# A fused transformer block: masked products moved to GpSimd, a count round split between two engines

## Chip, cores and metric

One core of a Trainium2 chip. The metric is the time of one execution on the device in microseconds (us). PE is TensorE (PEld its weight loads), DVE VectorE, ACT ScalarE, POOL GpSimd, SP SyncE.

## What is computed

The reference is two layers over x of shape 8 x 512 x 256; each adds an attention-like and a feed-forward part to a residual. The change touches only the attention of the first layer:

```
q, k, v = heads(xn @ Wq.T), heads(xn @ Wk.T), heads(xn @ Wv.T)      # 16 heads of 64
k, v    = concat(mem_k, k), concat(mem_v, v)                        # 64 memory keys in front
dots    = mix_heads(q @ k.T / 8, pre_proj)                          # heads blended, 16 x 16
dots    = where(key after query + 64, -max, dots)
kth     = top_k(dots, 64)[..., -1]                                  # the 64th largest of each row
attn    = softmax(where(dots < kth, -max, dots))
out     = mix_heads(attn, post_proj) @ v;  out @ Wout.T + bout
```

The rest is a feed-forward part with blockwise FP4 quantisation, then a second layer with a decaying scan (a convolution in the reference), a gated part and an INT4 dense part with a low-rank addition.

## The kernel before

**Tiling.** For each of 8 batches the 512 queries are cut into 8 groups of 64, taken in the order 7, 0, 5, 2, 6, 1, 4, 3. Group g sees up to `64 + 64 (g + 1)` keys. A group is a tile of 128 partitions (16 heads x 8 queries) by 8 blocks (`b`), and block b of group g has `keys(8 g + b) = 64 + 8 (8 g + b + 1)` columns, 72 to 576. The tile lies in a ring buffer `ring`, which holds six groups; a new group's scores may land only when an older group's last use (`turned`, L1299 and L1319) is over.

**Stages of a group.** `scores`: matmuls (L1004), evictions by ACT (L1019), DMAs that spread heads over partitions (L1028, SP's queue), clears by POOL (L1036), a matmul that blends heads (L1047), and ACT's exponentials into the ring (L1055), masked by POOL (L1068, L1070). So the ring holds positive numbers.

`search`: for each row a threshold `cur` is sought that a few less than 64 entries reach. A round counts, block by block, the entries on either side. On ACT a count is a Sign activation with an accumulator (L1085; ACTIVATE and ACTIVATION_READ_ACCUMULATOR are its two records); on DVE a comparison with an accumulator (L1089). `LONG` lists the rounds as (blocks counted on ACT, whether the step is made on POOL): three rounds with all eight blocks on ACT and the step on POOL, two rounds with all on DVE and the step on DVE. The step `narrow` (L1101 to L1147) turns counts into the next threshold with a chain of tiny instructions. ACT's sums are of signs and DVE's of ones; `base` turns the first into an excess over the aim. In a round that both share (`EDGE`, the first two groups of all), DVE's comparison is multiplied by -2 through a third operand `two` (L1091). `LAST` serves the last four groups. The last round's counts become `off`, the number that is still missing.

`soften`: for each block DVE makes a masked product, entries below the threshold and zeros for the others (L1155), and takes its eight largest (MAX8, L1158). `pick` (L1162 to L1169) selects the 64th largest from threshold, those eight and `off`, with a table `slots`. L1182 then zeroes what lies under it and sums the rest; its reciprocal (L1263) scales the mixing matrices on POOL (L1274).

`attend`: matmuls that mix heads and transpose (L1299, L1319), evictions (L1307, L1325), the product with v (L1343), then the output projection (L1367, L1371). Keys (L942), queries (L970) and values (L911) are made once per batch or pair of groups; in the drain the quantised feed-forward part of one batch is begun early (`early_mlp`, `begin_last`).

**Order of work.** Nothing is ordered by the hardware's timing alone: a planner (`Plan`) gets every operation with an engine, a modelled cost, its dependencies and the buffers that it takes and gives (`room`: so many of each name, taken in program order except for some). It plays the operations through; of those that an engine could start at about the same time it takes the one with the earliest due time. The result is the order of instructions on each engine, which is fixed. Due times are set by stage: `due(n, start, end)` spreads a stage's operations between two offsets, in groups, around group n's place on a clock (`DUE`, `START`, `MLP_DUE`, `BEGIN_DUE`). The second layer is planned separately, by the length of the chain behind each operation (its instructions all have line L276).

Of the kernel before, what the change touches and what calls it, by code (L numbers as in the profile page):

```python
# [8 lines left out]
F32 = mybir.dt.float32  # L9
U32 = mybir.dt.uint32  # L10
AF = mybir.ActivationFunctionType
ALU = mybir.AluOpType
# [3 lines left out]
P = 128  # L16
# [6 lines left out]
TOPK = 64  # L23
RB = 8
HH = H // 2
NB = N // RB
GB = 8
# [3 lines left out]
WD = [MEM + GR * (g + 1) for g in range(NG)]  # L31
# [10 lines left out]
def places(order):  # L42
# [16 lines left out]
AIM = LOW + 4.25  # L59
SPAN = 9  # L60

LONG = ((GB, True), (GB, True), (GB, True), (0, False), (0, False))

EDGE = ((GB // 2, False),) * (len(LONG) - 1) + ((0, False),)
LAST = ((GB, True),) * 3 + ((GB, False), (0, False))
# [7 lines left out]
FCH = ((0, 128), (128, 128), (256, 128), (384, 128), (512, 96), (608, 96))  # L73
FKC = len(FCH)
BLK = 16
MLP_DUE = (-6.89, -6.28)
BEGIN_DUE = (-4.57, -3.22)
START = dict(guess=(-7.0, -6.94), wvs=(-3.0, 6.46), out=(-2.39, -0.44), weights=(-6.86, -1.78), stores=(-3.17, 5.9))
DUE = dict(
    tokens=((-5.67, -1.96),),  # L80
    keys=((-4.8, -3.44),),
    queries=((-4.7, 2.49),),
    scores=((-2.64, -2.01), (-2.54, -2.24),),
    search=((6.0, 8.0), (6.0, 7.56),),
    soften=((-2.19, 5.82), (-6.06, -4.32),),
    values=((0.45, 3.36),),
    attend=((2.8, 3.05), (0.76, 6.89),),
    project=((-4.72, 6.69),),
)
FLT_MAX = 3.4028234663852886e38  # L90
MASKED = -1.0e30
# [555 lines left out]
def block_kernel(ctx: ExitStack, tc: tile.TileContext, a: dict, out: bass.AP):  # L647
    nc = tc.nc
# [51 lines left out]
    with ExitStack() as c0:  # L700
        keep = c0.enter_context(tc.tile_pool(name="keep", bufs=1))
# [9 lines left out]
        guess = keep.tile([P, NB], F32, name="guess")  # L711
# [5 lines left out]
        below = keep.tile([P, RB], F32, name="below")  # L717

        slots = keep.tile([P, SPAN], F32, name="slots")
        base = {}  # L720
        for na in sorted({na for na, _ in LONG + EDGE + LAST} - {0}):
            base[na] = keep.tile([P, NB], F32, name=f"base{na}")
        minus = keep.tile([P, GB], F32, name="minus")
        good = keep.tile([P, NB], F32, name="good")
        two = keep.tile([P, 1], F32, name="two")

        wvT = keep.tile([P, DC, H * DH], F32, name="wvT")
        woT = keep.tile([P, HC, D], F32, name="woT")
# [3 lines left out]
        scr = c0.enter_context(tc.tile_pool(name="scr", bufs=1))  # L732
# [7 lines left out]
        rp = c0.enter_context(tc.tile_pool(name="rp", bufs=2))  # L740
        wp = c0.enter_context(tc.tile_pool(name="wp", bufs=2))
# [5 lines left out]
        extra = keep.tile([P, 1840], F32, name="extra")  # L747
        with tc.tile_pool(name="prep", bufs=1) as prep, tc.tile_pool(name="prep_ps", bufs=1, space=PSUM) as pps:
            pl = Plan({})
            r = Straight(nc, pl, True)  # L750
# [81 lines left out]
            r.vector.tensor_scalar(below, cmask, -1.0, 1.0, ALU.mult, ALU.add)  # L832
            r.vector.tensor_scalar(cmask, cmask, MASKED, None, ALU.mult)
            for q in range(SPAN):
                r.gpsimd.memset(slots[:, q : q + 1], 2 * (TOPK - AIM - q))
            for na, to in base.items():
                r.gpsimd.memset(to, -2.0 * AIM)
                for ib in range(NB):
# [1 line left out]
                        r.gpsimd.memset(to[:, ib : ib + 1], keys(ib) - 2.0 * AIM)  # L840
            r.gpsimd.memset(good, 0.0)
            r.gpsimd.memset(minus, -1.0)
            r.gpsimd.memset(two, -2.0)
# [230 lines left out]
        def block(s, g, b):  # L1074
            return s[:, b, : keys(g * GB + b)]

        def count(g, s, cur, raw, b, na):


            on_act = b < na  # L1080
            src = block(s, g, b)
            thr = cur[:, 0, b : b + 1]
            junk = wp.tile([P, WD[-1]], I8, name=f"junk{int(on_act)}")[:, : src.shape[-1]]
            if on_act:
                nc.scalar.activation(  # L1085
                    junk, src, AF.Sign, bias=thr, scale=-1.0, accum_out=raw[:, b : b + 1]
                )
            elif na == 0:
                nc.vector.tensor_scalar(junk, src, thr, 0.0, ALU.is_ge, ALU.add, accum_out=raw[:, b : b + 1])  # L1089
            else:  # L1090
                nc.vector.scalar_tensor_tensor(  # L1091
                    junk, src, thr, two.to_broadcast([P, src.shape[-1]]), ALU.is_ge,
                    ALU.mult, accum_out=raw[:, b : b + 1],
                )

        def excess(eng, to, g, raw, na):

            if na == 0:
                eng.tensor_scalar(to, raw, 2.0, -2.0 * AIM, ALU.mult, ALU.add)
            else:  # L1100
                eng.tensor_tensor(to, base[na][:, g * GB : (g + 1) * GB], raw, ALU.subtract)  # L1101

        def narrow(g, w, k, na, on_pool):
# [46 lines left out]
        def under(g, s, cur, top, b):  # L1150
# [6 lines left out]
            )  # L1157
            nc.vector.max(out=top[:, b, 1:], in_=y)  # L1158

        def pick(cur, top, off, kth):  # L1160
# [35 lines left out]
        def search(pl, g, s, w, deps, rounds):  # L1196

            def begin():
                w["cur"] = cur = st.tile([P, 2, GB], F32, name="cur", bufs=14)
                nc.gpsimd.tensor_copy(cur[:, 0], guess[:, g * GB : (g + 1) * GB])  # L1200

            tail = pl.add("POOL", 0.3, begin, deps)
            for k, (na, on_pool) in enumerate(rounds):
                def open_():
                    w["raw"] = st.tile([P, GB], F32, name="raw", bufs=8)

                counts = []
                tail = pl.add("none", 0.0, open_, [tail])
                for b in range(GB):
                    def one_count(b=b, na=na):  # L1210
                        count(g, s, w["cur"], w["raw"], b, na)

                    n = keys(g * GB + b)
                    counts.append(
                        pl.add("ACT", 0.28 + 0.00083 * n, one_count, deps + [tail]) if b < na else
                        pl.add("DVE", 0.13 + 0.00105 * n, one_count, deps + [tail])
                    )

                def step(k=k, na=na, on_pool=on_pool):
                    if k < len(rounds) - 1:  # L1220
                        narrow(g, w, k, na, on_pool)
                    else:
                        w["off"] = st.tile([P, GB], F32, name="foff", bufs=4)
                        excess(nc.vector, w["off"], g, w["raw"], na)

                last = k == len(rounds) - 1
                tail = pl.add(
                    "POOL" if on_pool else "DVE",
                    0.2 if last else (0.9 if k == 0 else 4.6) if on_pool else 1.8 if k < len(rounds) - 2 else 2.1,
                    step, counts,  # L1230
                )
                deps = []
            return tail

        def soften(pl, g, s, w, tail, seen):

            def top0():
                w["top"] = small.tile([P, GB, SPAN], F32, name="top", bufs=2)

            op = tail  # L1240
            for b in range(GB):
                def un(b=b):
                    if b == 0:
                        top0()
                    under(g, s, w["cur"], w["top"], b)

                n = keys(g * GB + b)
                op = pl.add("DVE", 0.42 + 0.00154 * n, un, [op, tail])
            op = picked = pl.add("DVE", 0.9, lambda: pick(w["cur"], w["top"], w["off"], w["kth"]), [op])
            for b in range(GB):  # L1250
# [250 lines left out]
        def begin_last(pl, guard, ready):  # L1501
# [10 lines left out]


        pl = Plan(dict(
            scr=1, xnT=2, ps_m=3, ps_s=2, ps_a=2, ps_y=1, v=1, q=2, k0=1, k1=1, raw=4, rp=2, at=2, y=1,
            xset=1, xqT=2, hset=1, hT=2,
        ), ("scr", "ps_m", "ps_s", "ps_a", "ps_y"))
        groups = [(b, g) for b in range(B) for g in ORDERS[b]]
# [13 lines left out]


        r = Straight(nc, pl)
        hold = ["at", "at", "y", "ps_a", "ps_a", "ps_y", "xnT"]
        held_ = pl.add("none", 0.0, lambda: None, (), hold)
        banks = [ps_a.tile([P, 512], F32, name="ps_at") for _ in range(2)] + [ps_y.tile([P, 512], F32, name="ps_y")]
# [42 lines left out]
        junk = gates[:, 512:768].rearrange("p (j d) -> p j d", d=DH)  # L1580
# [62 lines left out]
        made = section("weights")  # L1643
# [3 lines left out]
        r.sync.dma_start(mk_d.rearrange("p (c m) -> p c m", m=MEM), kt[:, :, :MEM])  # L1647
        section("stores")
        pl.add("none", 0.0, lambda: None, [made, guessed, v_made, o_made], (), hold)

        kd = {}
        yt, ydone, judged, freed = {}, [], [None, None], {-1: made, -2: v_made, -3: o_made}
        for n, (b, g) in enumerate(groups):
# [15 lines left out]
            s = room(found[n][0], g)  # L1669
            last = n % NG == NG - 1  # L1670
# [4 lines left out]
            w = {}  # L1675
# [360 lines left out]
```

## Time and profile before

| | us |
|---|---|
| three runs: median (lowest to highest) | 2375.78 (2371.23 to 2377.31) |
| the profiled execution, its own time | 2370.63 |
| its span, first to last instruction | 2368.9 |
| first and last L1155 (masked product) start | 149.5, 1802.5 |
| busy PE, DVE, ACT, POOL | 2144.4, 2029.9, 1893.1, 1099.1 |

The mean granted TensorE clock was 0.96. The attention of the first layer takes the span from about 100 to 1820 us; the second layer and most of the feed-forward part follow. A row of the costliest groups reads: line, engine, operation, written and read tiles with shapes, count, then busy us and mean ns of one, then the engine's idle time just before them with what ended it.

### The profile page before, as it was taken

Reading aid. Unit: us, or ns where it says so; the run is one execution under the profiler, and the core shown is the slowest. Engines: PE = TensorE matmul, PEld = TensorE weight load, DVE = VectorE, ACT = ScalarE, POOL = GpSimd, SP = SyncE. Lnnn points to the kernel's source line nnn. Section 1 sums busy time; section 2 is a strip of 40 time slices with the busy share of each in tenths; the row PEclk is TensorE's granted clock in tenths of the full one; section 3 lists DMA queues with packets and bytes.
Section 4 is the critical chain, followed back from the end, with each engine's and each line's share of the span. In section 5 each row is a group of like instructions: output and inputs, shape, how many; then the busy total and the mean of one; then the engine's idle time right before and its main releaser. Section 6 shows DMA issues by size and latency. Waiting matters only on the chain. (4 is left out here: it accounts for less than half of the span.)

```text
span 2368.9 us, 57412 instructions
## 1 busy us (share of the span) xinstructions
PE 2144.4 (91%) x19629; PEld 1522.0 (64%) x19629; DVE 2029.9 (86%) x6462; ACT 1893.1 (80%) x5501; POOL 1099.1 (46%) x2678
## 2 busy tenths in 40 slices
PE   8788999989989999998999999999676889999998
PEld 7346675766767676676767667765455456665566
DVE  6998989988998998898899889979897788778764
ACT  4599999989999998998999899999963456444434
POOL 2424554445545554544455455545554544444330
PEclk9899999999999999999999999999888889999999
DMA  6552333253232424323332422444000310000000
GB/s 187 126 115 52 61 54 67 46 85 60 62 61 58 66 52 85 56 56 61 67 65 49 88 50 68 67 66 96 6 16 25 111 36 18 19 12 16 10 10 18
DMA packets 117156, 137.57 MB, mean 58 GB/s; under 512 B 20059, under 2 KB 102774, under 8 KB 116598
## 3 DMA queue, kind: packets, MB, share of 16 engines
q1 hardware_dynamic: 116854, 133.80, 28.0%
q8 instruction: 158, 2.59, 0.5%
q14 instruction: 144, 1.18, 0.2%
HBM read 27.32 MB, written 15.73 MB: 18 GB/s over the span
## 5 line engine op out<-in xcount | busy, mean ns | idle before, releaser
L1085 ACT ACTIVATE junk<-ring,cur 128x480 int8<-128x480 f32 (+33 forms) x1552 | 885.0, 586 | 11.9 <-POOL cur L1147 9.6
L1089 DVE TENSOR_SCALAR_CACHE_REDUCE junk<-ring,cur 128x520 int8<-128x520 f32 (+7 forms) x976 | 510.3, 540 | 78.2 <-POOL cur L1147 75.9
L1047 PE MATMUL ps_sc<-ring,blend 128*128 128x264 f32 (+50 forms) x1152 | 363.7, 436 | 44.6 <-DMA ring<-raw 20.6
L1319 PE MATMUL ps_at<-mixd,ring 128*128 128x128 f32 x2560 | 353.8, 287 | 22.1 <-POOL mixd L1274 12.5
L1319 PEld LDWEIGHTS ps_at<-mixd,ring 128*128 128x128 f32 x2560 | 320.3, 197 | 61.0 <-POOL mixd L1274 20.5
L1085 ACT ACTIVATION_READ_ACCUMULATOR junk<-ring,cur 128x1 f32 x1552 | 337.2, 217 | 0.0
L1155 DVE SCALAR_TENSOR_TENSOR y<-ring,cur 128x520 f32<-128x520 f32 (+56 forms) x512 | 307.3, 600 | 7.3
L1047 PEld LDWEIGHTS ps_sc<-ring,blend 128*128 128x128 f32 x1152 | 193.3, 195 | 163.6 <-ACT ring L1055 56.5
L1182 DVE SCALAR_TENSOR_TENSOR ring<-ring,kth 128x520 f32<-128x520 f32 (+56 forms) x512 | 280.6, 556 | 1.1
L1158 DVE MAX8 top<-y 128x8 f32<-128x520 f32 (+56 forms) x512 | 255.7, 499 | 17.6
L1019 ACT COPY raw<-ps_mi 128x284 f32<-128x284 f32 (+15 forms) x576 | 223.1, 430 | 38.3 <-DMA ring<-raw 28.6
L1004 PE MATMUL ps_mi<-kt,qT 64*32 64x284 f32 (+15 forms) x4608 | 230.3, 442 | 15.4 <-ACT raw L1019 13.9
L1055 ACT ACTIVATE ring<-ps_sc 128x272 f32<-128x272 f32 (+33 forms) x576 | 229.0, 426 | 16.8 <-PE ps_sc L1047 14.7
L1343 PEld LDWEIGHTS ps_y<-at,v 128*64 128x64 f32 (+1 forms) x6144 | 196.1, 138 | 58.3 <-ACT at L1325 19.8
L1343 PE MATMUL ps_y<-at,v 128*64 128x64 f32 (+1 forms) x6144 | 220.4, 225 | 3.9 <-ACT at L1325 2.8
L1137 POOL TENSOR_TENSOR by<-gap,minus 128x8 f32<-128x8 f32 x124 | 212.7, 1715 | 9.7
L1325 ACT COPY at<-ps_at 128x512 f32<-128x512 f32 x320 | 191.2, 600 | 29.5 <-PE ps_at L1319 28.0
L1101 POOL TENSOR_TENSOR cur<-base,raw 128x8 f32<-128x8 f32 x186 | 46.4, 249 | 329.2 <-ACT junk L1085 326.1
L1274 POOL TENSOR_TENSOR mixd<-mix,rden 128x256 f32<-128x256 f32 x256 | 168.8, 684 | 18.7 <-DVE rden L1263 16.4
L276 PE MATMUL ps_gu<-big,ring 128*128 128x352 f32 x448 | 149.2, 478 | 15.4 <-DVE hid L276 8.4
L1036 POOL MEMSET ring<- 128x56 f32 (+6 forms) x448 | 34.7, 124 | 247.1 <-DMA ring<-raw 244.2
L276 PE MATMUL ps_l<-ring,w 128*128 128x512 f32 (+2 forms) x288 | 124.3, 575 | 21.2 <-DVE u L276 15.7
(306 smaller groups left out, 3889.8 us busy)
## 6 DMA issues: line engine op xcount, KB each, us to landing
ring<-raw SPq DMA_DIRECT2D x32, 288.0 KB
ring<-raw SPq DMA_DIRECT2D x32, 284.0 KB
ring<-raw SPq DMA_DIRECT2D x32, 256.0 KB
ring<-raw SPq DMA_DIRECT2D x32, 252.0 KB
ring<-raw SPq DMA_DIRECT2D x32, 224.0 KB
ring<-raw SPq DMA_DIRECT2D x32, 220.0 KB
ring<-raw SPq DMA_DIRECT2D x32, 192.0 KB
ring<-raw SPq DMA_DIRECT2D x32, 188.0 KB
```

The costliest lines, as they stand in the source:

```text
L276: call = lambda: fn(*a, **k)
L1004: nc.tensor.matmul(some[u][j * SUB : (j + 1) * SUB, : n1 - n0], q["T"][rows, 4 * rnd + j, side, sub::2], kt[rows, 4 * rnd + j, n0:n1], sta ...
L1019: nc.scalar.copy(k["raw", 2 * rnd + u][:, n0:n1], k["of", rnd, n0][u][:, : n1 - n0])
L1047: nc.tensor.matmul(ps[:, : n1 - n0], blend.rearrange("p k i -> p (k i)"), s[:, b, n0:n1], start=True, stop=True,)
L1055: nc.scalar.activation(s[:, b, n0:n1], k["pb", b][i][:, : n1 - n0], AF.Copy if plain else AF.Exp, scale=DH ** -0.5)
L1085: nc.scalar.activation(junk, src, AF.Sign, bias=thr, scale=-1.0, accum_out=raw[:, b : b + 1])
L1089: nc.vector.tensor_scalar(junk, src, thr, 0.0, ALU.is_ge, ALU.add, accum_out=raw[:, b : b + 1])
L1155: nc.vector.scalar_tensor_tensor(y, src, cur[:, 0, b : b + 1], src, ALU.is_lt, ALU.mult)
L1158: nc.vector.max(out=top[:, b, 1:], in_=y)
L1182: nc.vector.scalar_tensor_tensor(src, src, kth[:, b : b + 1], e, ALU.is_ge, ALU.mult, accum_out=den[:, b : b + 1])
L1319: nc.tensor.matmul(pt[:n, b * P : (b + 1) * P], s[:, 4 * j + b, col : col + n], w["mix"][j][:, b, :], start=True, stop=True,)
L1343: nc.tensor.matmul(w["py"][j * DH : (j + 1) * DH, q * GR : (q + 1) * GR], vs[c][:n, k * DH : (k + 1) * DH], ats[c][:n, k, :], start=(c == ...
```

## The change

- `LONG`'s third round: `(GB, True)` becomes `(GB // 2, True)`: blocks 0 to 3 are counted on ACT, 4 to 7 on DVE; the step stays on POOL.
- A count on DVE is always the plain comparison (L1089's form). In rounds that both engines share, `excess` first multiplies the eight sums by `turned` (1 for ACT's, -2 for DVE's).
- The last round counts what is below the threshold (`is_lt` for `is_ge`); `fewer` (keys less 64) is subtracted to give `off`, and `slots` holds 0 to 8.
- For blocks 1, 3, 5 and 7 that last comparison writes a bf16 mask (four buffers in `extra`) where the others write a junk tile. POOL multiplies the block by its mask (`lift`, two buffers), and DVE only takes MAX8 of the product. Blocks 0, 2, 4, 6 keep L1155, and come first.
- The junk tiles have one buffer each, not two. Mask and lift buffers are free once the weights are prepared (`made`).
- All due offsets have other values.

```diff
-LONG = ((GB, True), (GB, True), (GB, True), (0, False), (0, False))
+LONG = ((GB, True), (GB, True), (GB // 2, True), (0, False), (0, False))
+LIFTED = (1, 3, 5, 7)
+MASK, MASKS, LIFTS = 288, 4, 2
...
-MLP_DUE = (-6.89, -6.28)
-BEGIN_DUE = (-4.57, -3.22)
-START = dict(guess=(-7.0, -6.94), wvs=(-3.0, 6.46), out=(-2.39, -0.44), weights=(-6.86, -1.78), stores=(-3.17, 5.9))
+MLP_DUE = (-6.45, -5.91)
+BEGIN_DUE = (-4.09, 0.33)
+START = dict(guess=(-4.88, -3.55), wvs=(4.09, 4.72), out=(-3.0, -0.49), weights=(-2.6, 1.34), stores=(-5.75, -3.05))
 DUE = dict(
-    tokens=((-5.67, -1.96),),
-    keys=((-4.8, -3.44),),
-    queries=((-4.7, 2.49),),
-    scores=((-2.64, -2.01), (-2.54, -2.24),),
-    search=((6.0, 8.0), (6.0, 7.56),),
-    soften=((-2.19, 5.82), (-6.06, -4.32),),
-    values=((0.45, 3.36),),
-    attend=((2.8, 3.05), (0.76, 6.89),),
-    project=((-4.72, 6.69),),
+    tokens=((-0.07, 7.33),),
+    keys=((-3.85, -0.22),),
+    queries=((-1.82, 0.71),),
+    scores=((-0.79, -0.79), (-1.08, -0.71),),
+    search=((3.02, 5.15), (3.67, 5.48),),
+    soften=((-1.81, 3.71), (-3.2, -1.01),),
+    values=((4.52, 5.0),),
+    attend=((3.89, 5.34), (-1.77, 6.48),),
+    project=((-1.29, 0.63),),
 )
...
+            for ib in range(NB):
+                r.vector.memset(fewer[:, ib : ib + 1], float(keys(ib) - TOPK))
+            for na, to in turned_.items():
+                r.gpsimd.memset(to[:, :na], 1.0)
+                r.gpsimd.memset(to[:, na:], -2.0)
...
+        def lower(g, s, cur, raw, b, mask):
+            src = block(s, g, b)
+            if mask is None:
+                mask = wp.tile([P, WD[-1]], I8, name="junk0", bufs=1)
+            nc.vector.tensor_scalar(
+                mask[:, : src.shape[-1]], src, cur[:, 0, b : b + 1], 0.0, ALU.is_lt, ALU.add, accum_out=raw[:, b : b + 1]
+            )
+        def lift(g, s, b, k):
+            src = block(s, g, b)
+            k["y"] = y = lifted()[:, : src.shape[-1]]
+            nc.gpsimd.tensor_tensor(y, src, k["mask"][:, : src.shape[-1]], ALU.mult)
...
-                nc.vector.scalar_tensor_tensor(
-                    junk, src, thr, two.to_broadcast([P, src.shape[-1]]), ALU.is_ge,
-                    ALU.mult, accum_out=raw[:, b : b + 1],
-                )
...
+                if na < GB:
+                    eng.tensor_tensor(raw, raw, turned_[na], ALU.mult)
                 eng.tensor_tensor(to, base[na][:, g * GB : (g + 1) * GB], raw, ALU.subtract)
...
+                    if last:
+                        op = pl.add("DVE", 0.13 + 0.00105 * n, one_lower, deps + [tail], ["mask"] * (b in LIFTED))
+                        counts.append(op)
+                        if b in LIFTED:
...
+                            w["raised", b] = pl.add("POOL", 0.15 + 0.002 * n, one_lift, [op], ["lift"], ["mask"])
+                        continue
...
-            for b in range(GB):
+            for b in sorted(range(GB), key=lambda b: b in LIFTED):
...
+                def tops(b=b):
+                    nc.vector.max(out=w["top"][:, b, 1:], in_=w["lift", b]["y"])
...
-                op = pl.add("DVE", 0.42 + 0.00154 * n, un, [op, tail])
+                if b in LIFTED:
+                    op = pl.add("DVE", 0.28 + 0.0005 * n, tops, [op, tail, w["raised", b]], (), ["lift"])
+                else:
+                    op = pl.add("DVE", 0.42 + 0.00154 * n, un, [op, tail])
```

More of the change, by code (lines that the diff above doesn't have):

```diff
@@ L719, in block_kernel @@
         slots = keep.tile([P, SPAN], F32, name="slots")
-        base = {}
+        base, turned_ = {}, {}
         for na in sorted({na for na, _ in LONG + EDGE + LAST} - {0}):
             base[na] = keep.tile([P, NB], F32, name=f"base{na}")
+            if na < GB:
+                turned_[na] = keep.tile([P, GB], F32, name=f"turned{na}")
         minus = keep.tile([P, GB], F32, name="minus")
         good = keep.tile([P, NB], F32, name="good")
-        two = keep.tile([P, 1], F32, name="two")
+        fewer = keep.tile([P, NB], F32, name="fewer")
         wvT = keep.tile([P, DC, H * DH], F32, name="wvT")
@@ L834, in block_kernel @@
             for q in range(SPAN):
-                r.gpsimd.memset(slots[:, q : q + 1], 2 * (TOPK - AIM - q))
+                r.gpsimd.memset(slots[:, q : q + 1], float(q))
             for na, to in base.items():
@@ L842, in block_kernel @@
             r.gpsimd.memset(minus, -1.0)
-            r.gpsimd.memset(two, -2.0)
+            for ib in range(NB):
[3 more added lines that the diff above has]
+                r.gpsimd.memset(to[:, na:], -2.0)
             pl.tails()
@@ L1075, in block, with mask_of, lifted @@
             return s[:, b, : keys(g * GB + b)]
+        def mask_of():
+            turn_m[0] += 1
+            at_ = MASK * (turn_m[0] % MASKS)
+            return extra[:, at_ : at_ + MASK].bitcast(BF16)
+        def lifted():
+            turn_l[0] += 1
+            return lifts[turn_l[0] % LIFTS]
+        def lower(g, s, cur, raw, b, mask):
[9 more added lines that the diff above has]
+            nc.gpsimd.tensor_tensor(y, src, k["mask"][:, : src.shape[-1]], ALU.mult)
         def count(g, s, cur, raw, b, na):
@@ L1082, in count @@
             thr = cur[:, 0, b : b + 1]
-            junk = wp.tile([P, WD[-1]], I8, name=f"junk{int(on_act)}")[:, : src.shape[-1]]
+            junk = wp.tile([P, WD[-1]], I8, name=f"junk{int(on_act)}", bufs=1)[:, : src.shape[-1]]
             if on_act:
@@ L1087, in count @@
                 )
-            elif na == 0:
+            else:
                 nc.vector.tensor_scalar(junk, src, thr, 0.0, ALU.is_ge, ALU.add, accum_out=raw[:, b : b + 1])
-            else:
-                nc.vector.scalar_tensor_tensor(
-                    junk, src, thr, two.to_broadcast([P, src.shape[-1]]), ALU.is_ge,
-                    ALU.mult, accum_out=raw[:, b : b + 1],
-                )
         def excess(eng, to, g, raw, na):
@@ L1100, in excess @@
             else:
+                if na < GB:
+                    eng.tensor_tensor(raw, raw, turned_[na], ALU.mult)
                 eng.tensor_tensor(to, base[na][:, g * GB : (g + 1) * GB], raw, ALU.subtract)
@@ L1158, in under @@
             nc.vector.max(out=top[:, b, 1:], in_=y)
+        turn_m, turn_l = [0], [0]
+        lifts = [extra[:, MASK * MASKS : MASK * MASKS + WD[-1]], wp.tile([P, WD[-1]], F32, name="lift", bufs=1)]
         def pick(cur, top, off, kth):
@@ L1208, in search @@
                 tail = pl.add("none", 0.0, open_, [tail])
+                last = k == len(rounds) - 1
                 for b in range(GB):
@@ L1211, in one_count, with one_lower, one_lift @@
                         count(g, s, w["cur"], w["raw"], b, na)
-                    n = keys(g * GB + b)
+                    def one_lower(b=b):
+                        if b in LIFTED:
+                            w["lift", b] = {"mask": mask_of()}
+                            lower(g, s, w["cur"], w["raw"], b, w["lift", b]["mask"])
+                        else:
+                            lower(g, s, w["cur"], w["raw"], b, None)
+                    n = keys(g * GB + b)
+                    if last:
+                        op = pl.add("DVE", 0.13 + 0.00105 * n, one_lower, deps + [tail], ["mask"] * (b in LIFTED))
+                        counts.append(op)
+                        if b in LIFTED:
+                            def one_lift(b=b):
+                                lift(g, s, b, w["lift", b])
+                            w["raised", b] = pl.add("POOL", 0.15 + 0.002 * n, one_lift, [op], ["lift"], ["mask"])
+                        continue
                     counts.append(
@@ L1223, in step @@
                         w["off"] = st.tile([P, GB], F32, name="foff", bufs=4)
-                        excess(nc.vector, w["off"], g, w["raw"], na)
-                last = k == len(rounds) - 1
+                        nc.vector.tensor_tensor(
+                            w["off"], w["raw"], fewer[:, g * GB : (g + 1) * GB], ALU.subtract
+                        )
                 tail = pl.add(
@@ L1245, in un @@
                     under(g, s, w["cur"], w["top"], b)
+                def tops(b=b):
+                    nc.vector.max(out=w["top"][:, b, 1:], in_=w["lift", b]["y"])
                 n = keys(g * GB + b)
-                op = pl.add("DVE", 0.42 + 0.00154 * n, un, [op, tail])
+                if b in LIFTED:
+                    op = pl.add("DVE", 0.28 + 0.0005 * n, tops, [op, tail, w["raised", b]], (), ["lift"])
+                else:
+                    op = pl.add("DVE", 0.42 + 0.00154 * n, un, [op, tail])
             op = picked = pl.add("DVE", 0.9, lambda: pick(w["cur"], w["top"], w["off"], w["kth"]), [op])
@@ L1514, in block_kernel @@
         pl = Plan(dict(
-            scr=1, xnT=2, ps_m=3, ps_s=2, ps_a=2, ps_y=1, v=1, q=2, k0=1, k1=1, raw=4, rp=2, at=2, y=1,
+            scr=1, xnT=2, ps_m=3, ps_s=2, ps_a=2, ps_y=1, v=1, q=2, k0=1, k1=1, raw=4, rp=2, at=2, y=1, mask=MASKS, lift=LIFTS,
             xset=1, xqT=2, hset=1, hT=2,
@@ L1534, in block_kernel @@
         r = Straight(nc, pl)
+        pl.add("none", 0.0, lambda: None, (), ["mask"] * MASKS + ["lift"] * LIFTS)
         hold = ["at", "at", "y", "ps_a", "ps_a", "ps_y", "xnT"]
@@ L1649, in block_kernel @@
         pl.add("none", 0.0, lambda: None, [made, guessed, v_made, o_made], (), hold)
+        pl.add("none", 0.0, lambda: None, [made], (), ["mask"] * MASKS + ["lift"] * LIFTS)
         kd = {}
```

## The prediction

> **What bounds it now.** I read the 40 slices first, then busy time by stage, the costliest groups, the waits of the middle stage, and forms one by one. The slices of the page:
>
> ```profile
> PE   8788999989989999998999999999676889999998
> DVE  6998989988998998898899889979897788778764
> ACT  4599999989999998998999899999963456444434
> POOL 2424554445545554544455455545554544444330
> ```
>
> From slice 3 to 27 ACT stands at 9, PE and DVE just under it, POOL at half. In the last quarter, the layers behind attention, ACT is half idle; the change leaves them alone. By stage (columns: window, length, then PE, PEld, DVE, ACT, POOL busy with instructions):
>
> ```profile
> 100.00:200.00 100.00, 80.65 (x719) 47.18 (x719) 94.15 (x344) 90.95 (x279) 32.22 (x89) 0.95 0.43 92
> 200.00:1600.00 1400.00, 1333.84 (x14789) 967.72 (x14790) 1250.46 (x4499) 1338.57 (x4186) 699.41 (x2068) 0.98 0.35 63
> 1700.00:1820.00 120.00, 77.98 (x674) 63.31 (x674) 112.54 (x335) 65.91 (x181) 64.48 (x94) 0.80 0.03 10
> ```
>
> L1155 runs 437 times in 200 to 1600, eight per group, so 54.6 groups pass there, **25.6 us each**. Per group ACT is busy 24.5 us, PE 24.4, DVE 22.9, POOL 12.8. A busy PE counts matmuls that wait in its pipe; laid end to end at the pace of their dense stretches (0.112 us from start to start for 128 columns, 0.216 for 256, 0.246 for L1047's mean of 288, about 0.68 for L1004's sets of 16, 1.08 for L1343's of 32) its passes need some 1270 us, 23.3 per group. So ACT bounds the stage with 96% and 1.1 us idle per group, and PE and DVE are 5 to 7% behind it. The waits agree: when PE is held up it is mostly by ACT's results (L1055, L1085, L1325), seldom the other way. DVE bounds the drain from 1700 to 1820 (112.5 of 120 us) and the entry from 100 to 200.
>
> The lines of the search:
>
> ```profile
> L1085 ACT ACTIVATE junk<-ring,cur 128x480 int8<-128x480 f32 (+33 forms) x1552 | 885.0, 586 | 11.9 <-POOL cur L1147 9.6
> L1089 DVE TENSOR_SCALAR_CACHE_REDUCE junk<-ring,cur 128x520 int8<-128x520 f32 (+7 forms) x976 | 510.3, 540 | 78.2 <-POOL cur L1147 75.9
> L1155 DVE SCALAR_TENSOR_TENSOR y<-ring,cur 128x520 f32<-128x520 f32 (+56 forms) x512 | 307.3, 600 | 7.3
> L1158 DVE MAX8 top<-y 128x8 f32<-128x520 f32 (+56 forms) x512 | 255.7, 499 | 17.6
> L276 POOL TENSOR_TENSOR q_lo_h<-q_lo_h,q_v_h 128x704 f32<-128x704 f32 x28 | 51.5, 1840 | 125.3 <-DVE q_lo_h L276 88.1 <-DVE ri L276 14.7 <-DVE ln_mv L276 14.2
> ```
>
> L1085 is ACT's largest piece. DVE's only large idle time, 76 us, waits for POOL's narrowing step (L1147). POOL idles, but what it owes the others is late already.
>
> **The change, part by part**, per group of the 58 that use LONG.
>
> *Third round.* Four counts, b = 4 to 7 with 340 columns on average, leave ACT. In the timeline one count begins 0.67 us before the next ACT instruction at 456 columns and 0.40 at 136: 0.57 at 340. ACT: 24.5 - 4 x 0.57 = **22.2**. They arrive on DVE, where L1089 begins 0.34 us before its successor at 208 columns and 0.39 at 256; with its mean of 0.54 at 324 columns less 0.06 overlap, 0.50: **+2.0**. The plain count needs a small POOL product with `turned` before L1101, by L1101's row (0.25 us) +0.3 with its gap. It lengthens the narrowing chain, in the timeline 4.7 us from L1101 to L1147.
>
> *Masked products.* Four L1155 leave DVE; with the pause before MAX8, 0.60 to 0.63 each: **-2.5**. The four MAX8 stay. POOL gets four two-input products of 328 columns. No row shows fp32 times bf16 on POOL. Nearest rows: with a broadcast operand 256 columns take 0.684 (L1274) and 704 take 1.461 (L276), so 0.81 at 328; with two full operands 0.865 (L393) and 1.840 (above), so 1.02. Both operands are full: I take 1.02, **+4.1**, POOL 12.8 + 4.1 + 0.3 = 17.2 of 25.
>
> *The last count* compares the other way and writes int8 or bf16. L1089 writes one byte and L1155 four, and both need 0.75 us at 520 columns, so the width costs nothing: 0 (up to +0.1). `foff` as a subtraction: 0.24 to 0.17, nothing. One junk buffer for two: its writers share an engine in order, nothing. The masks lie in `extra`, last used at 136.8 us; the first L1155 starts at 149.5: hidden, up to 13 us once if that margin goes.
>
> *POOL against DVE.* Look at L1155 by form:
>
> ```profile
> L1155 DVE SCALAR_TENSOR_TENSOR y<-ring,cur 128x288 f32<-128x288 f32 x7 | 5.9, 842 | 0.2
> L1155 DVE SCALAR_TENSOR_TENSOR y<-ring,cur 128x456 f32<-128x456 f32 x7 | 5.3, 757 | 0.0
> L1089 DVE TENSOR_SCALAR_CACHE_REDUCE junk<-ring,cur 128x288 int8<-128x288 f32 x14 | 7.0, 501 | 0.0
> L1089 DVE TENSOR_SCALAR_CACHE_REDUCE junk<-ring,cur 128x456 int8<-128x456 f32 x14 | 9.6, 683 | 2.4 <-POOL cur L1147 2.1
> ```
>
> The count with one tensor input grows with its columns; the product with two is longer at 288 columns than at 456, and single ones reach 1.61 us (median 0.60). Those stand beside POOL instructions, and in turn L1146 on POOL takes 0.62 instead of 0.20 beside L1182. Over all, L1155 is 0.06 us above L1089: some 0.5 us of DVE per group today. What a lift adds has no row. Below: 0, and even -0.2, as half of L1155 goes. Above: every lift stops DVE for its length, +4.1. I take **+0.4**, near today's row, since the lifts add a third to POOL's reading but are longer than most of it and fall beside one-input counts. DVE: 22.9 + 2.0 - 2.5 + 0.4 = **22.8**. The Trainium skill ("SBUF — State Buffer", Who interferes with whom) states this as a rule: a VectorE instruction with two SBUF inputs and a GpSimd instruction that reads SBUF exclude each other for a whole instruction. It speaks against the move; if every lift cost DVE its full length, the sum would have DVE at 26.5 us and some 50 us more than now; the one-input rows agree with the exception that it makes for them.
>
> *Waits that are new.* `lift` has two buffers, so the third and fourth lift wait on POOL until DVE has taken MAX8 of the first and second, which come behind four L1155/L1158 pairs. Queued behind a waiting lift are another group's narrowing, L1036 clears, L1068 masks and L1274 products; their users are ACT, DVE and PE. Cost 0 if other groups' work covers it, up to 3.5 us per group (four pairs at 1.1, less one lift).
>
> *Entry and drain.* EDGE's 32 counts lose the second operand (0.68 to 0.54, 4 us of DVE), `fewer` adds 64 tiny memsets on DVE (about 6 us at the 0.1 us of POOL's row, partly in idle time): 0 together. In the DVE-bound drain the last four groups lose 16 L1155, 9.6 us; part returns as POOL round trips: **-6** (0 to -10).
>
> *Due offsets* reorder every queue, and no row prices an order. Gain at most the 61 us that ACT idles in the stage; loss: in four windows at batch turns ACT is busy for 43.6, 44.5, 44.4 and 42.7 of 50 us, 6 us short each; as much again at eight turns would be 48. I take 0.
>
> **The sum.** ACT 22.2, DVE 22.8, PE 23.3: PE is late next, and DVE right behind. Today the bound engine loses 1.1 us per group with its followers 1.2 or more behind; with three within 1.1 of one another I give 1.2: 24.5 per group, -1.1 x 58 = -64. Ends: 0.4 lost (23.7, -110), or 2.3 lost (no gain). With -6 from the drain the profiled 2370.6 us (span 2368.9 and 1.7 around it) becomes 2301. The median of the runs, 2375.8, is 5 us above that execution: **2306**. The skill ("Trainium Kernel Development and Optimization", Performance Expectations) tells one to judge TensorE by the busy share of weight loads, not of matmuls; that is 17.7 us per group here. By it PE would not be next; DVE's 22.8 would, and the time would be about 30 us lower. I keep 23.3, since dense stretches show the passes themselves that far apart.
>
> **Rivals.**
> 1. *PE and DVE fill up nearly fully*, 23.3 to 23.7 per group: -110 to -133, so 2235 to 2260. For it: PE is mostly held by ACT, whose queue shortens, and a third round split over two engines ends sooner. Against: no engine now exceeds 96%.
> 2. *Nothing comes of it*: the ring is full, and SP's queue waits 406 us for L1299 and L1319 to free its rooms; if the length of a group's passage, not the load, sets the pace, ACT's relief turns into idle time: 2368 to 2383. Against: a full ring is also what a bound ACT leaves behind.
> 3. *POOL's queue makes it slower.* One mechanism: lifts that wait for DVE (MAX8, or a two-input instruction) stand ahead of another group's narrowing, and the next counts start late on both engines. Place: L1101 to L1147 behind a lift. Price: up to 3.5 us of waiting per group. It decides once it adds more than the 1.1 us gained to the 25.6; at the full 3.5, (3.5 - 1.1) x 58 = +139; at half, 1.75 - 1.1 = 0.65, +38: 2414. For it: DVE's 76 us of waiting for L1147. Against: POOL at 67%, and six groups in flight.
>
> **Chances.** Forecast and its neighbourhood (2260 to 2368): 0.65. Rival 1: 0.13. Rival 2: 0.08. Rival 3: 0.14. A measurement of this kernel tells about 0.3% from no change, so faster means below 2368.7: 0.78; same 0.08; slower 0.14. The range takes in half of the cases beyond each end: 2250 to 2390.
>
> **What would show it.** Right: ACT below 22.5 us per group and idle, L1085 at 1320 (1552 less 232), the 200 to 1600 stage holding 57 groups, PE's busy share up, the drain shorter. The lifts near 1.0 us; above 1.4 the exclusion is dearer than I took. Wrong: DVE's or ACT's idle time before the counts behind L1147 grown past 2 us per group (rival 3); ACT's idle time up and groups no faster (rival 2); L1155 and L1182 means up by over 0.1 us (the exclusion). The most fragile steps are the 1.2 us of loss between three near-equal engines and the zero for the due offsets.

## The result and the profile after

The changed kernel takes **2393.44 us** (median of six runs, 2389.92 to 2396.9), the kernel before 2376.26 (six runs, 2371.23 to 2377.5). The ratio is 1.0075 [1.0061, 1.0088]: slower by 17 us, where the prediction said 2306 in a range from 2250 to 2390. The profiled execution took 2389.92 us, its span 2388.2.

The slices of the page after, in the order of those shown of before:

```profile
PE   8788899999999999999999999999668789989998
DVE  6998989998898898889899889988788798787764
ACT  4599899989979988997998899799963456444434
POOL 2426656656656665765666466566564554444330
```

POOL has risen by a digit, and ACT shows sevens and eights where it stood at 9. By stage (columns: window, length, then PE, PEld, DVE, ACT, POOL busy with instructions, then the granted clock):

```profile
100.00:200.00 100.00, 80.37 (x681) 45.56 (x681) 89.55 (x335) 88.19 (x256) 32.61 (x91) 0.93 0.39 88
200.00:1600.00 1400.00, 1333.97 (x14689) 961.86 (x14688) 1249.05 (x4710) 1266.18 (x3720) 878.39 (x2322) 0.99 0.35 63
1700.00:1820.00 120.00, 73.33 (x635) 59.02 (x634) 106.81 (x314) 79.08 (x217) 74.14 (x122) 0.80 0.04 10
```

In the middle stage ACT is busy 72 us less than before and POOL 179 more, while DVE is where it was (1250.46 before). So the loads moved much as intended. The pace did not: L1184, now four per group, runs 216 times there, 54.0 groups against 54.6, **25.9 us each** against 25.6. The last L1214 (the step behind the search) starts at 1826.8 us, 18.5 later than its twin L1182 before (1808.3), and from there to the end both need 561 us. So 18.5 of the 19.3 us between the two spans lie ahead of it, in the attention.

The lines of the search:

```profile
L1117 ACT ACTIVATE junk<-ring,cur 128x136 int8<-128x136 f32 (+38 forms) x1320 | 751.5, 569 | 49.2 <-POOL cur L1149 19.7
L1121 DVE TENSOR_SCALAR_CACHE_REDUCE junk<-ring,cur 128x392 int8<-128x392 f32 (+9 forms) x728 | 400.0, 549 | 68.0 <-POOL cur L1176 55.5
L1184 DVE SCALAR_TENSOR_TENSOR y<-ring,cur 128x520 f32<-128x520 f32 (+31 forms) x256 | 145.9, 570 | 2.3
L1107 POOL TENSOR_TENSOR lift<-ring,extra 128x528 f32<-128x528 f32 (+15 forms) x128 | 105.7, 826 | 86.7 <-DVE extra L1099 46.4
L1184 DVE SCALAR_TENSOR_TENSOR y<-ring,cur 128x456 f32<-128x456 f32 x8 | 5.4, 672 | 0.0
L278 POOL TENSOR_TENSOR q_lo_h<-q_lo_h,q_v_h 128x704 f32<-128x704 f32 x28 | 51.5, 1841 | 124.6 <-DVE q_lo_h L278 87.3 <-DVE ri L278 14.7 <-DVE ln_mv L278 14.3
```

L1117 fell from 1552 to 1320 as foreseen, a lift takes 0.83 us, and the masked product on DVE became shorter (0.57 from 0.60). DVE's idle time before its counts is 68.0 us (78.2 before). Nothing here explains a loss. But for POOL no engine is fuller. ACT's idle time in the stage rises from 61 to 134 us, but in small pieces: its longest sum of waits, for a DMA, is 24.5 us (22.9 before). What is missing is mostly inside the busy time. Compare two neighbouring counts on ACT, in the timeline (columns: start, length) of before, then of after:

```profile
830.01 0.74 ACT L1085 ACTIVATE junk<-ring,cur 128x504 int8<-128x504 f32 x1
830.62 0.23 ACT L1085 ACTIVATION_READ_ACCUMULATOR junk<-ring,cur 128x1 f32 x1
830.71 0.74 ACT L1085 ACTIVATE junk<-ring,cur 128x512 int8<-128x512 f32 x1
```

```profile
827.01 0.72 ACT L1117 ACTIVATE junk<-ring,cur 128x504 int8<-128x504 f32 x1
827.64 0.19 ACT L1117 ACTIVATION_READ_ACCUMULATOR junk<-ring,cur 128x1 f32 x1
827.86 0.72 ACT L1117 ACTIVATE junk<-ring,cur 128x512 int8<-128x512 f32 x1
```

Before, the next count begins 0.09 us after the accumulator's read began; after, it begins 0.03 us after that read has ended: 0.85 us from count to count for 0.70. The same on DVE, before and then after:

```profile
609.25 0.62 DVE L1089 TENSOR_SCALAR_CACHE_REDUCE junk<-ring,cur 128x432 int8<-128x432 f32 x1
609.78 0.09 DVE L1089 DVE_READ_ACCUMULATOR junk<-ring,cur 128x1 f32 x1
609.78 0.67 DVE L1089 TENSOR_SCALAR_CACHE_REDUCE junk<-ring,cur 128x440 int8<-128x440 f32 x1
```

```profile
1012.29 0.65 DVE L1121 TENSOR_SCALAR_CACHE_REDUCE junk<-ring,cur 128x416 int8<-128x416 f32 x1
1012.86 0.08 DVE L1121 DVE_READ_ACCUMULATOR junk<-ring,cur 128x1 f32 x1
1012.98 0.65 DVE L1121 TENSOR_SCALAR_CACHE_REDUCE junk<-ring,cur 128x424 int8<-128x424 f32 x1
1013.56 0.08 DVE L1121 DVE_READ_ACCUMULATOR junk<-ring,cur 128x1 f32 x1
1013.56 0.27 DVE L1298 MAX8 top<-lift 128x8 f32<-128x112 f32 x1
```

In the last fence both cases stand together: another count starts 0.69 us behind a count of 416 columns, a MAX8 that writes elsewhere 0.58 behind one of 424. Sorted by what comes next, over the whole stage, with 0.87 ns (ACT) and 1.04 ns (DVE) per column taken off the distance from start to start (medians):

| | before | after | before with one junk tile |
|---|---|---|---|
| ACT, next is a count | 0.27 us | 0.41 (491 pairs) | 0.41 (534) |
| ACT, next is something else | 0.27 | 0.28 | 0.28 |
| DVE, next is a count into the same tile | 0.13 | 0.26 (222 pairs) | 0.26 (205) |
| DVE, next is something else | 0.13 | 0.13 | 0.13 |

So **the theory**: the junk tiles, cut from two buffers to one each, make a count wait for the write of the count before it on its own engine. Price on ACT: 491 x 0.136 = 67 us in the stage, 1.2 per group, where the change was to gain 1.1. (Some 18 of the 67 us are gaps of 0.03 us; the rest shows as busy time, since the accumulator's read no longer lies beside the next count.) The Trainium skill ("VectorE: DVE Perf Modes", The DRAIN you can't avoid) says of eight copies on VectorE that a semaphore behind each costs nothing extra, since the next waits for the pipe to empty in any case. The counts of this case differ: the one-tile wait adds 0.12 us on DVE. On ACT, of which that section does not speak, it adds 0.14. **The rivals**: the lifts hold POOL's queue (the prediction's rival 3), DVE is slowed by POOL's reads, PE is the bound, or the new due offsets order the queues worse.

### The profile page after: what moved, and what is told of

It reads as the page before. It is cut to its first block, busy times and chain, and to the rows that moved or that the text cites. A ratio compares the mean times of both kernels' runs of the same rounds, so it can differ in the third digit from the quotient of the medians.

```text
span 2388.2 us, 57719 instructions
## 1 busy us (share of the span) xinstructions
PE 2157.0 (90%) x19629; PEld 1523.4 (64%) x19629; DVE 2026.3 (85%) x6742; ACT 1835.3 (77%) x5037; POOL 1306.8 (55%) x2993
## 5 line engine op out<-in xcount | busy, mean ns | idle before, releaser
L1117 ACT ACTIVATE junk<-ring,cur 128x136 int8<-128x136 f32 (+38 forms) x1320 | 751.5, 569 | 49.2 <-POOL cur L1149 19.7
L1121 DVE TENSOR_SCALAR_CACHE_REDUCE junk<-ring,cur 128x392 int8<-128x392 f32 (+9 forms) x728 | 400.0, 549 | 68.0 <-POOL cur L1176 55.5
L1055 PE MATMUL ps_sc<-ring,blend 128*128 128x264 f32 (+49 forms) x1152 | 359.0, 431 | 23.7 <-ACT ring L1063 11.5
L1375 PEld LDWEIGHTS ps_at<-mixd,ring 128*128 128x128 f32 x2560 | 315.1, 194 | 77.9 <-ACT at L1381 31.6
L1375 PE MATMUL ps_at<-mixd,ring 128*128 128x128 f32 x2560 | 346.2, 284 | 17.4 <-ACT at L1381 13.0
L1214 DVE SCALAR_TENSOR_TENSOR ring<-ring,kth 128x520 f32<-128x520 f32 (+56 forms) x512 | 281.4, 563 | 1.3
L1117 ACT ACTIVATION_READ_ACCUMULATOR junk<-ring,cur 128x1 f32 x1320 | 259.5, 197 | 0.0
L1012 PE MATMUL ps_mi<-kt,qT 64*32 64x284 f32 (+15 forms) x4608 | 233.3, 438 | 17.2 <-ACT raw L1027 15.4
L1399 PE MATMUL ps_y<-at,v 128*64 128x64 f32 (+1 forms) x6144 | 223.2, 226 | 16.3 <-ACT at L1381 9.8
L1330 POOL TENSOR_TENSOR mixd<-mix,rden 128x256 f32<-128x256 f32 x256 | 154.5, 633 | 69.3 <-PE ps_at L1355 32.3
L278 PE MATMUL ps_gu<-big,ring 128*128 128x352 f32 x448 | 147.4, 473 | 15.4 <-DVE hid L278 8.3
L1107 POOL TENSOR_TENSOR lift<-ring,extra 128x528 f32<-128x528 f32 (+15 forms) x128 | 105.7, 826 | 86.7 <-DVE extra L1099 46.4
L1423 PE MATMUL ps_mi<-woT,y 128*128 128x256 f32 x512 | 131.3, 415 | 21.3 <-ACT y L1413 17.2
L1184 DVE SCALAR_TENSOR_TENSOR y<-ring,cur 128x520 f32<-128x520 f32 (+31 forms) x256 | 145.9, 570 | 2.3
L278 PE MATMUL ps_l<-ring,w 128*128 128x512 f32 (+2 forms) x288 | 123.4, 572 | 21.3 <-DVE u L278 15.8
L1099 DVE TENSOR_SCALAR_CACHE_REDUCE extra<-ring,cur 128x528 bf16<-128x528 f32 (+31 forms) x256 | 139.3, 545 | 0.0
```

Source lines behind the costliest of these rows:

```text
L278: call = lambda: fn(*a, **k)
L1012: nc.tensor.matmul(some[u][j * SUB : (j + 1) * SUB, : n1 - n0], q["T"][rows, 4 * rnd + j, side, sub::2], kt[rows, 4 * rnd + j, n0:n1], sta ...
L1055: nc.tensor.matmul(ps[:, : n1 - n0], blend.rearrange("p k i -> p (k i)"), s[:, b, n0:n1], start=True, stop=True,)
L1117: nc.scalar.activation(junk, src, AF.Sign, bias=thr, scale=-1.0, accum_out=raw[:, b : b + 1])
L1214: nc.vector.scalar_tensor_tensor(src, src, kth[:, b : b + 1], e, ALU.is_ge, ALU.mult, accum_out=den[:, b : b + 1])
L1375: nc.tensor.matmul(pt[:n, b * P : (b + 1) * P], s[:, 4 * j + b, col : col + n], w["mix"][j][:, b, :], start=True, stop=True,)
```

## The experiments

Ratios are to the kernel before on the same chip (2374.4 to 2375.4 us).

**Due offsets and parts.** Four kernels: before with after's offsets, after with before's offsets, and with these offsets each part by itself.

```diff
+MLP_DUE = (-6.45, -5.91)   # and BEGIN_DUE, START, DUE: all of after (e1, upon before)
-MLP_DUE = (-6.45, -5.91)   # all offsets of before (e2, e3, e4, upon after)
-LIFTED = (1, 3, 5, 7)      # e3
+LIFTED = ()
-LONG = ((GB, True), (GB, True), (GB // 2, True), (0, False), (0, False))   # e4, with NEAR 0.08 -> 0.07
+LONG = ((GB, True), (GB, True), (GB, True), (0, False), (0, False))
```

> The kernel before with the new due offsets and nothing else. Theory A (POOL's queue: the lifts cost what the split gains): the offsets matter little, 2370 to 2385. Theory B (the order of work sets the time, the parts little): the offsets were not set for this work, 2390 to 2420. Theory C (PE and the ring set the pace, whatever ACT does): within 0.5% of 2376.

> The changed kernel with the old due offsets: split and lifts both in. Theory A: about as the changed kernel, 2385 to 2400. Theory B: far off on either side, since these offsets were not set for it: below 2370 or above 2410. Theory C: 2370 to 2395.

> Old due offsets, the third round split, every masked product on DVE (no lifts). Theory A: the gain of the split without POOL's queue, though DVE has 2.0 us more per group: 2350 to 2375. Theory B: 2376 to 2420 by order alone. Theory C: DVE rises to 24.9 us per group and bounds with PE: 2385 to 2410.

> Old due offsets, half of the masked products on POOL, the third round all on ACT; the planner's window for near starts is 0.07 us instead of 0.08. ACT keeps 24.5 us per group, DVE falls to 20.8. Theory A: slower than 2376 by POOL's queue, 2390 to 2430. Theory B: anywhere within 1% of 2376. Theory C: 2370 to 2385, as neither ACT nor PE changes.

Three of the four came out slower than any theory had them. Measured: new offsets alone 2466.25, 1.0386 [1.0371, 1.0401]; both parts with the old offsets 2452.28, 1.0332 [1.0318, 1.0346]; split alone 2485.34, 1.0466 [1.0451, 1.048]; lifts alone 2475.73, 1.0421 [1.0407, 1.0435]. The new offsets make the old loads 91 us slower and the new loads 59 us faster (2452.28 less 2393.44). An order belongs to its loads; neither is worth a number by itself. And since each of the last three carries the one-tile wait, none says what a part is worth.

**What holds the changed kernel.** One engine at a time is made lighter, with the order of the queues kept (the branch for the exact search is switched off where counts or products are cut). The lifts work on 8 columns after the first group, so most of the masked product of four blocks is left out; ACT's counts of rounds 1 and 2 take half of their columns; L1214 takes half of its columns; the output projection makes one of its eight matmuls.

```diff
-            nc.gpsimd.tensor_tensor(y, src, k["mask"][:, : src.shape[-1]], ALU.mult)
+            some = src.shape[-1] if turn_l[0] <= 4 else 8
+            nc.gpsimd.tensor_tensor(y[:, :some], src[:, :some], k["mask"][:, :some], ALU.mult)
...
+            if on_act and k < 2:
+                src = src[:, : src.shape[-1] // 2]
...
-                for q in range(HH):
-                    nc.tensor.matmul(po, yt["y"][:, q, :], woT[:, q, :], start=(q == 0), stop=(q == HH - 1))
+                for q in range(1):
+                    nc.tensor.matmul(po, yt["y"][:, q, :], woT[:, q, :], start=True, stop=True)
```

> The changed kernel, same order, with the lifts cut to 8 columns after the first group: POOL 3 us lighter per group and nothing to exclude DVE with. The thresholds' eight candidates are stale, so results are wrong, and the last test for the exact path is switched off. Theory A: 2330 to 2365, below the kernel before. Theory C: 2385 to 2393. Theory D: 2365 to 2385.

> The changed kernel, same order, with the counts of the first two rounds on ACT over half of their columns: ACT 2.3 us lighter per group, as much again as the split took off. Counts and thresholds are wrong, and the test for the exact path is switched off. Theories A and C: 2383 to 2393, as ACT idles 9% already. Theory D: 2355 to 2380.

> The changed kernel, same order, with the final zeroing and summing (L1214) over half of each block: DVE 1.35 us lighter per group, and fewer columns in two-input instructions. Weights and sums are incomplete. Theory A: 2365 to 2385. Theory C: 2385 to 2393. Theory D: 2350 to 2380.

> The changed kernel, same order on every engine, with PE lighter by about 1.5 us per group: of the output projection's eight matmuls (two passes each) only the first is made, so the attention's output is incomplete. Theory C (PE and what it waits for is the next bound): 2393 falls by 50 to 95, to 2300 to 2345. Theory A (POOL's queue and its exclusion with DVE): 2375 to 2393. Theory D (no engine: each waits in a fixed order for the others): a part of it, 2350 to 2375.

Measured: lifts 2380.3, 1.002 [1.0011, 1.003], 13 us less than after; ACT 2343.13, 0.9866 [0.985, 0.9881], 50 less and below both expectations, for 140 us of counts cut (their busy time, 751.5 to 611.6); DVE 2379.77, 1.0016 [1.0004, 1.0028], 14 less for 88 cut (281.4 to 193.8); PE 2392.12, 1.0068 [1.0055, 1.0081], nothing. So the length of the lifts and their reads beside DVE are 13 of the 87 us between 2306 and 2393. The cut lifts still wait for DVE in POOL's queue, 113 us of the stage for 87 in after. What settles these waits is rival 3's own place, the counts that wait for POOL's narrowing (columns: us in total, times, longest), in before and then in after:

```profile
DVE junk L1089 <- POOL cur L1147: 74.5, 34, 6.7
ACT junk L1085 <- POOL cur L1147: 4.1, 5, 0.9
```

```profile
DVE junk L1121 <- POOL cur L1176: 50.0, 41, 4.1
ACT junk L1117 <- POOL cur L1149: 18.3, 7, 3.8
```

They wait 68 us in after for 79 in before, so POOL's queue isn't where the loss is. Nor is it PE's load (its granted clock fell with it, see the end), and DVE gives little. ACT gives most, although it shows more idle time than before.

**The junk tile by itself.** Both directions: before with one tile, and after with two for ACT. The second lies in `extra`, made 32 words longer, with two `gap` buffers fewer; the order of every engine's queue stays. DVE keeps one.

```diff
-            junk = wp.tile([P, WD[-1]], I8, name=f"junk{int(on_act)}")[:, : src.shape[-1]]
+            junk = wp.tile([P, WD[-1]], I8, name=f"junk{int(on_act)}", bufs=1)[:, : src.shape[-1]]
...
+            turn_j[on_act] += 1
+            if on_act and turn_j[on_act] % 2:
+                at_ = MASK * MASKS + 0
+                junk = extra[:, at_ : at_ + 144].bitcast(I8)[:, : src.shape[-1]]
+            else:
+                junk = wp.tile([P, WD[-1]], I8, name=f"junk{int(on_act)}", bufs=1)[:, : src.shape[-1]]
```

> The kernel before with one junk tile per engine instead of two, and nothing else. Theory E: about 640 counts on ACT stand right behind another and lose 0.14 us each, 250 on DVE lose 0.12, on a stage that ACT bounds: 2430 to 2480. Theories A and D: the tiles' writers run in order on one engine, so nothing: 2371 to 2380.

> The changed kernel, same order, with ACT's counts writing to two junk tiles in turn again (the second lies in `extra`; 12 `gap` tiles instead of 14 make room); DVE's counts keep one. Theory E (a count right behind a count waits for the one junk tile: 0.41 instead of 0.27 us besides its columns in the changed kernel's trace, some 575 times on ACT): 78 us of ACT go, of which the order may give back a third to all: 2315 to 2370, faster than both. Theory A (POOL's queue is what eats the gain) and theory D (an order planned with wrong costs, wherever they are): ACT idles 9% anyway, 2380 to 2393.

Measured: before with one tile on each of the two engines 2444.26, 1.0285 [1.027, 1.0299], **70 us slower**, DVE's wait included; after with two for ACT **2333.41**, 0.9824 [0.9808, 0.9839], 60 us faster than after and 41 than before. It beats both kernels. The same two counts in its timeline:

```profile
802.91 0.70 ACT L1122 ACTIVATE extra<-ring,cur 128x504 int8<-128x504 f32 x1
803.51 0.19 ACT L1122 ACTIVATION_READ_ACCUMULATOR extra<-ring,cur 128x1 f32 x1
803.60 0.71 ACT L1122 ACTIVATE junk<-ring,cur 128x512 int8<-128x512 f32 x1
```

Written tiles alternate, and the distance is back at 0.69 us. Its middle stage, and that of before with one tile:

```profile
200.00:1600.00 1400.00, 1353.47 (x15130) 982.22 (x15132) 1294.06 (x4893) 1259.35 (x3860) 906.45 (x2400) 1.00 0.37 65
```

```profile
200.00:1600.00 1400.00, 1297.75 (x14245) 938.03 (x14245) 1223.65 (x4356) 1336.60 (x4022) 670.83 (x1971) 0.98 0.33 60
```

The mended kernel, after with two tiles for ACT, passes 56.3 groups (225 of its masked products), 24.9 us each, and ACT is busy 1259.35 / 56.3 = 22.4 us per group. Before with one tile passes 52.8, and ACT's busy time is the same as in before (1338.57) for 1.8 groups fewer: most of the wait is booked as busy time.

**Was ACT the bound of the kernel before?** The same cuts of ACT and PE, on before.

> The kernel before, same order, with ACT's counts of the first two rounds over half of their columns: ACT 2.3 us lighter per group, as much as the split takes off. Counts and thresholds are wrong, and the test for the exact path is switched off. If ACT bounds the stage as the prediction read it: 2235 to 2310 (most of 143 us). If the fixed order gives back a third, as the same cut did in the changed kernel (50 of 143): 2315 to 2340.

> The kernel before, same order, with one of the output projection's eight matmuls: PE 1.5 us lighter per group, the attention's output incomplete. If PE is next behind ACT: 2360 to 2376. If PE matters nowhere, as in the changed kernel: 2372 to 2380.

Measured: ACT 2368.28, 0.9964 [0.9953, 0.9976], **6 us**, less than either expectation, for 149 cut (885.0 to 736.4; the records overlap, so ACT's whole busy time falls by less, 1893.1 to 1790.6); PE 2385.63, 1.0036 [1.0023, 1.0049], slower. The stage of the first:

```profile
200.00:1600.00 1400.00, 1336.56 (x14793) 970.19 (x14794) 1244.82 (x4498) 1251.90 (x4190) 697.45 (x2066) 0.98 0.36 63
```

ACT is 87 us less busy, and no more groups pass (x4498 on DVE, x4499 before). The junk wait on ACT and DVE costs 70 us; ACT made faster gains 6. So 96% busy was no sign that relief of ACT alone would help with the order as it was.

**What is left in the mended kernel.** It gains 41 us where the sum said 70. Its parts one at a time (no split; no lifts, with NEAR 0.08 -> 0.09), and the two cuts again (each leaves out what it did above).

> The kernel after with two junk tiles in turn for ACT (2333 us) and the third round's counts all on ACT again, so that of the change the lifted products and the due offsets are left. ACT gets back 2.3 us per group and DVE gives 2.0. If ACT's load still sets the pace, some 2.3 x 58 = 130 us come back at most, and at least the 43 us of the gain: 2376 to 2460. If the lifts carry the gain and the split does little: 2325 to 2345. The due offsets were found for the split, so an order that fits worse can add to either.

> The same kernel with two junk tiles for ACT, the products of all eight rows on DVE again (no lifts; the window of the order widened by a hundredth of a step), so that the split and the due offsets are left. DVE gets back 2.5 us per group and would stand at 25.3: if DVE then sets the pace, some 25.9 per group, 2400 to 2430. If the lifts do nothing for the pace: 2325 to 2345.

> The mended kernel whose products on GpSimd work on 8 columns after the first group (leaves out most of the masked product of four rows; the branch for the exact search is switched off). GpSimd falls by about 2.6 us per group. If GpSimd's queue, or what it takes from DVE, is what keeps the mended kernel 27 us short of the prediction's sum: 2305 to 2315, as the same cut gave 13 us with one junk tile, or more. If not: 2328 to 2336.

> The mended kernel with ACT's counts of the first two rounds on half of their columns (leaves out half of these counts; the branch for the exact search is switched off). ACT falls by some 2.4 us per group, 143 us in all. If ACT still sets the pace: 40 to 60 us less, 2275 to 2295, as with one junk tile. If ACT no longer does, as in the kernel before, where the same cut gave 6: 2320 to 2333.

Measured: without the split 2434.71, 1.0261 [1.0241, 1.0281]; without the lifts 2443.2, 1.0293 [1.0266, 1.032]; lifts cut 2317.04, 0.9759 [0.9727, 0.979]; ACT cut 2332.52, 0.9821 [0.9798, 0.9845]. Leaving out 148 us of ACT's counts (748.3 to 600.5) now gives nothing (2333.41 with them), so a lighter ACT is worth nothing in the mended kernel any more. The stage of that run:

```profile
200.00:1600.00 1400.00, 1356.87 (x15101) 983.56 (x15096) 1292.04 (x4880) 1166.24 (x3848) 903.07 (x2400) 0.99 0.37 65
```

ACT is 93 us less busy than in the mended kernel. PE is busy for 1357 of the 1400 us, 97%, and in the mended kernel for 1353: a larger share than ACT's 96% in the kernel before. No run makes PE lighter there. The lifts hold 16 us. Neither part pays alone under these offsets: both are 60 us and more slower than before, though each run mixes the part's load with offsets set for both. For no lifts, 2443 is above the 2400 to 2430 that DVE's load gave.

## Why the prediction was wrong

**The failed step** is a sentence: "One junk buffer for two: its writers share an engine in order, nothing." It took the order on the engine to make the second buffer needless, but the two tiles were what let one count start while the other finished. The term is not 0 but 67 us on ACT in the stage by the pairs; 60 us come back with the second tile for ACT, and 70 are lost when before gets a single one on ACT and DVE. That is 60 of the 87 us between 2306 and 2393. With it mended the sum's 2306 stands against 2333, inside the range. Partly that nearness is luck, since a premise of the sum failed as well, the first of the points below.

The other steps, in order:
- *ACT bounds the stage.* Not as put. Lighter ACT gained 6 us in before. The loads were read rightly, but by these runs the pace was that of fixed queues laid for those loads: a part that takes longer than the order assumed delays, one that takes less waits. That the mended kernel gained because loads and offsets changed together is argued: no run has the changed loads with two tiles for ACT and the old offsets.
- *Third round*, ACT to 22.2: after had 1266.18 / 54.0 = 23.4, of which (67 - 18) / 54.0 = 0.9 are the part of the waits that shows as busy time; mended 22.4. Right within 0.3.
- *Lifts* at 1.02 us: 0.83 and 0.87. POOL 16.3 per group for 17.2. The lower bound (0.81) was the better row.
- *DVE* at 22.8: 1249.05 / 54.0 = 23.1, some 0.3 of it junk waits (222 x 0.124 / 54.0 = 0.5 per group, 0.2 of that in gaps).
- *Exclusion* at +0.4: long instructions hardly felt it (L1214 0.563 for L1182's 0.556; L1184 shorter). What rose on DVE are small steps, most with two inputs (one of the narrowing from 0.17 to 0.24, `hot` from 0.23 to 0.33), 0.3 per group over five such rows (16.6 us in 54 groups). The skill's rule of mutual exclusion ("SBUF — State Buffer", Who interferes with whom), taken at full length, would by the prediction's estimate have put DVE at 26.5; the trace sides with the small value.
- *Waits on the lift buffers*, 0 to 3.5: POOL waits 38.7 us there in the stage (34.8 and 3.9 for the two buffers), 0.7 per group, and the counts behind the narrowing wait no longer than before. Small, near the low end. (Without the lifts' length 13 us come back, with these waits still there.)
- *Due offsets* at 0: they are -59 us on the new loads (with one junk tile) and +91 on the old ones. A term that belongs to the sum as a whole, not a zero.
- *The 1.2 us of loss* at a pitch of 24.5: mended 24.9. The missing 0.4 x 58 = 23 us are most of the 27 between 2306 and 2333. The lifts account for up to 16. DVE's single junk tile (27 us of waits in the stage) is the next suspect; a second one for DVE wasn't tried.
- *Rivals.* Rival 2 came nearest in time. Its mechanism, relief that turns into idle time, is what lighter ACT shows in the kernel before (2368.28, 87 us less busy); in the changed kernel the new wait on ACT itself was added to it. Rival 3's sign was right and its mechanism wrong: the counts wait no longer for the narrowing than before. Rival 1 would have needed more than the mended kernel gave.

Of the signs that the prediction named, ACT's idle time and the groups per stage were right to watch, but none looked at the distance from one count to the next, where the loss was.

**Open**: what sets the pace of the kernel before, where lighter ACT gains next to nothing and lighter PE, at a lower clock, nothing; DVE wasn't made lighter there. SP's queue waits of 406 us before and 455 after for L1355 and L1375 (L1299 and L1319) fit a ring that is full, but no run enlarged it. And of the mended kernel's 27 us, some 11 stay without a cause that a run has shown; PE, 97% busy there, DVE's single tile and the lifts' waits on POOL are the candidates.

## What to carry to other kernels

When a change takes a buffer away from a result that nobody reads, look at its writers: if two of them follow each other on one engine, measure their distance from start to start in the trace of before, and price a wait for the first one's end: here 0.14 us on ACT and 0.12 on DVE per pair, where the accumulator's reads took 0.19 and 0.08. Such a wait stands mostly in the busy time, and its gaps of 0.03 us in no list of waits, so divide busy time by the work done (us per group), and sort instructions by what follows them. In a kernel whose queues are laid out in advance, a high busy share does not tell what relief is worth: cut the work of one engine with the order kept, before a step is priced as a gain.

## What the runs showed of the hardware

- A count with an accumulator may overlap its successor's start: on ACT 0.27 us besides 0.87 ns per column from start to start, on DVE 0.13 besides 1.04. If the successor writes the same tile, about 0.41 and 0.26, at all widths from 72 to 568 columns.
- A lighter PE got a lower clock. With one of the projection's eight matmuls the mean granted clock fell from 0.960 to 0.940 in before and from 0.962 to 0.944 in after. The stage of the first:

```profile
200.00:1600.00 1400.00, 1281.09 (x14369) 901.74 (x14370) 1240.42 (x4482) 1333.55 (x4159) 684.39 (x2047) 0.96 0.34 63
```

PE is busy 53 us less, the clock stands at 0.96 for 0.98, and the kernel is 11 us slower; that the clock is the reason is argued, not shown. The skill ("TensorE: Matmul & The Clock Gate", Part 1) has the clock follow how busy PE has lately been, and these runs agree in direction.
- A two-input product of fp32 and bf16 on POOL takes 0.83 to 0.87 us at 328 columns in the mean, less than the 1.02 estimated from L393's and L278's two full fp32 operands. With it in the kernel DVE's long instructions were longer by 0.01 us or less in the mean.
